# Moving 352 weight loads from SyncE's queue to ScalarE's in a fused attention and FFN kernel

## The chip, the cores and the metric

The kernel runs on one core of one Trainium2 chip. The metric is the device time of one execution in microseconds (us). A core has five engines that run side by side, each with its own instruction stream: TensorE (PE, matrix products; its weight loads are listed apart as PEld), VectorE (DVE), ScalarE (ACT), GpSimd (POOL) and SyncE (SP). Data moves between DRAM and the on-chip memory (SBUF) by DMA transfers, which an engine issues as an instruction of its stream and which sixteen DMA engines carry out. Matrix products land in PSUM, which here is used as eight banks. Engines wait for each other, and for transfers, on semaphores; an engine works through its instructions in order, so that whatever stands behind a waiting instruction waits too.

## The reference

Sixteen sequences of 512 tokens of width 512 go through one attention layer and one feed-forward layer (FFN):

```python
x = x + layernorm(attn(layernorm(x)))
x = x + layernorm(ffn(layernorm(x)))

def attn(h):                               # 16 heads of 32
    q = h @ Wq_down.T @ Wq_up.T
    c = h @ Wkv_down.T
    k, v = c @ k_up[h], c @ v_up[h]        # per head
    s = q @ k.T * SCALE - slope[h] * |i - j|
    return softmax(where(i >= j, s, -inf)) @ v @ Wo.T

def ffn(h):                                # I = 1408
    gate, up = split(h @ W_gu.T)           # W_gu, W_down: 4-bit codes x scales per 128 inputs
    y = (silu(gate) * up) @ W_down.T
    return y / sqrt(mean(y * y) + 1e-6)
```

## The kernel before

**The loop.** The kernel goes through 16 batches (one sequence each). A batch has an attention part of 16 pieces (4 groups of heads times 4 blocks of query rows) and an FFN part of 11 blocks of 128 inner columns. Nothing is written as a loop of the chip: every instruction of all batches stands in the program once.

**The order.** The kernel first lists all work as tasks. A task names the engine or engines that could run it, with two times for each (how long the engine is busy, when the result is there), a due time in units of a batch, and the buffers it reads and writes. The class `Plan` (L71) then puts all tasks in one order by a model of its own: over and over it takes, of all tasks that are ready, the one that could start first; with equal starts the one with the earlier due time. The order that comes out is the order of each engine's instructions. Three of its rules matter here. A task starts after its inputs with a hop of 150 ns between engines, 350 ns towards TensorE (`HOP`, `SLACK`). If the input is a transfer issued by SyncE and the task is TensorE's, the hop is 1000 ns (`LANDED`). A task of SyncE that needs a buffer starts no sooner than 4000 ns after that buffer came free (`VACANT`), so that its queue is not held by a wait for the buffer. The real times on the chip may differ from the model; the order stays.

**Transfers.** A load by SyncE is priced by `dma(us)` (L253): 450 ns of the issuing engine, and `us` until the data is there. In SyncE's stream stand, per batch from the second on: 4 loads of `xl` and 4 of `x` (rows of the input, L389 and L840); for each of the 16 attention pieces a store of the transposed probabilities to DRAM (`pd`, L793) and four loads that bring them back turned (`pT`, L798); for each of the 4 groups a store of the reciprocal row sums (`rd`, L742) and four loads that spread them (`rb`, L747); and for each of the 11 FFN blocks two loads of unpacked weights (`wi`, L889), one for gate and one for up. The first batch turns its probabilities on TensorE instead (L774) and unpacks the 4-bit codes once, into the DRAM tensor `w_gu` (stores at L562), from which all 352 loads of `wi` read. Results leave through GpSimd's queue (L983).

**The FFN block.** A load of `wi` is 256 KB: 128 partitions of 512 values. Four buffers take them in turn. Each is the weight operand of eight matmuls (L898): four slices of the input, each as a coarse and a fine part (`x2`) that add up in one PSUM bank. ScalarE empties the banks of the slices 0 and 2 with the scale (L912), VectorE those of 1 and 3, adding to the same tile (L919); GpSimd adds the two tiles (L925). Then come ScalarE's tanh (L932), VectorE's product for silu (L935) and GpSimd's product with up (L939), whose result `hT` is the operand of the down projection on TensorE (L947). In the order that the planner makes, the FFN of one batch lies among the attention of the next: TensorE alternates between gate/up products, down products (`py`), scores (`s`, L681) and attention products (`po`, L818). ScalarE's exponentials (L708) take the row minima `nmx` that VectorE finds (L693); VectorE also transposes the probabilities block by block (L791) before the store to DRAM.

**What the load waits for.** A load of `wi` waits for the matmuls that last read its buffer (a semaphore that TensorE raises) and, in the trace, often for an older transfer (one of eight semaphores that transfers raise).

The planner's rule for a start, and the load, are the lines that the change touches:

Of the kernel before, what the change touches and what calls it, by code (L numbers as in the profile page):

```python
# [29 lines left out]
PE, ACT, DVE, POOL, SP = "PE", "ACT", "DVE", "POOL", "SP"  # L30
# [29 lines left out]


class Task:
    __slots__ = ("on", "fn", "due", "deps", "wait", "next", "bufs", "end", "mode", "seq", "eng", "drains")

    def __init__(self, on, fn, due, mode, seq):
        self.on, self.fn, self.due, self.mode, self.seq = on, fn, due, mode, seq
        self.deps, self.next, self.bufs = set(), [], []
        self.wait, self.end, self.eng = 0, None, None


class Plan:  # L71
# [67 lines left out]
    def run(self, window):  # L139
        clock = {e: 0.0 for e in (PE, ACT, DVE, POOL, SP)}  # L140
        ready = {e: [] for e in clock}
        mode = "full"
        rest = sorted((t for t in self.tasks if PE in t.on), key=lambda t: t.due)
        at = 0
        for t in self.tasks:
            if t.wait == 0:
                for e in t.on:
                    ready[e].append(t)
        order = []

        def start(t, e, kept):
            s = clock[e]
            for d in t.deps:
                hop = 0.0 if d.eng == e else self.SLACK if e == PE else self.HOP
                if d.eng == SP and e == PE:
                    hop = self.LANDED
                s = max(s, d.end + hop)
            need = {}
            for b in t.bufs:
                if b.pool is not None and b.slot is None:  # L160
                    need[b.pool] = need.get(b.pool, 0) + 1
            for k, n in need.items():
                f = self.free[k]
                if len(f) < n + (kept if k == "bank" else 0):
                    return None
                s = max(s, f[n - 1][0] + (self.VACANT if e == SP and f[n - 1][0] else 0.0))
            return s

        left = len(self.tasks)
        while left:  # L170
            while at < len(rest) and rest[at].end is not None:
                at += 1
            limit = rest[at].due + window if at < len(rest) else float("inf")
            best = None
            for e, ts in ready.items():
                now, mine, kept = clock[e], None, 0
                if e == PE and ts:

                    first = min(ts, key=lambda t: (t.due, t.seq))
                    kept = sum(b.pool == "bank" and b.slot is None for b in first.bufs)  # L180
                for t in ts:
                    if t.due > limit:
                        continue
                    s = start(t, e, 0 if e != PE or t is first else kept)
                    if s is None:
                        continue
                    due = t.due
                    if e != PE:
                        due -= self.EARLY if t.drains else 0.0
                    elif t.mode != "full":  # L190
                        due -= self.STAY[mode != "full", t.mode == mode]
                    key = (max(s, now), due, t.seq)
                    if mine is None or key < mine[0]:
                        mine = key, t
                if mine is not None:

                    key, t = mine
                    cand = (key[0], key[1], key[2], e, t)
                    if best is None or cand[:3] < best[:3] or (
                        cand[:3] == best[:3] and t.on[e][1] < t.on[best[3]][1]  # L200
                    ):
                        best = cand
            assert best is not None, "the buffers do not suffice"
            s, _, _, e, t = best
            for o in t.on:
                ready[o].remove(t)
            for b in t.bufs:
                if b.pool is not None and b.slot is None:
                    b.slot = self.free[b.pool].pop(0)[1]
            busy, done = t.on[e]  # L210
            if e == PE and t.mode != mode:
                busy, done, mode = busy + self.SWITCH, done + self.SWITCH, t.mode
            clock[e] = s + busy
            t.end, t.eng = s + done, e
            for b in t.bufs:
                b.left -= 1
                b.last = max(b.last, t.end)
                if b.left == 0 and b.pool is not None:
                    self.free[b.pool].append((b.last + self.SLACK, b.slot))
                    self.free[b.pool].sort()  # L220
            for n in t.next:
                n.wait -= 1
                if n.wait == 0:
                    for o in n.on:
                        ready[o].append(n)
            order.append(t)
            left -= 1
        self.length = max(clock.values())
        return order
# [19 lines left out]
def pe(ns):  # L249
    return ns, ns + 250  # L250


def dma(us):  # L253
    return 450.0, us * 1000.0

# [1 line left out]
def attn_ffn_kernel(  # L259
# [15 lines left out]
    nc = tc.nc  # L275
# [41 lines left out]
    task = plan.task  # L317
# [91 lines left out]
    for w, src, due in ((w_qd, wqd, -0.38), (w_qu, wqu_t, -0.37)):  # L409
# [5 lines left out]
            due, writes=[w],  # L415
# [462 lines left out]
    def ffn(m):  # L878
# [3 lines left out]
        for i in range(NI):  # L882
            accs = []
            for half, kind in enumerate("gu"):
                acc = buf(kind, f"{kind}_{b}_{i}")
                add = buf("sum", f"{kind}2_{b}_{i}")
                wi = buf("wi", f"wi_{b}_{i}_{half}")
                task({SP: dma(4.5)},
                     lambda e, i=i, half=half, wi=wi: nc.sync.dma_start(  # L889
                         wi.t.bitcast(F32), w_gu[i, half]),  # L890
                     at - 0.1, reads=[(gu, (i, half))], writes=[wi])
                for c in range(ND):
                    o = half * ND + c
                    pm = buf("bank", f"p{kind}_{b}_{i}_{c}")

                    def f(e, wi=wi, c=c, pm=pm):
                        for n in range(2):
                            nc.tensor.matmul(  # L898
                                pm.t,
                                wi.t[:, c * P : (c + 1) * P],  # L900
                                m.x2.t[:, 1 - n, c, :],
                                start=n == 0,
                                stop=n == 1,
                            )

                    s = s_gu.t[:, i * NGU + o : i * NGU + o + 1]
                    to = acc if c < 2 else add
                    task({PE: pe(460)}, f, at, reads=[wi, m.x2], writes=[pm], hold=[to])
                    if c % 2 == 0:
                        task(  # L910
                            {ACT: act(512, 80)},
                            lambda e, to=to, pm=pm, s=s: nc.scalar.activation(  # L912
                                to.t, pm.t, AF.Copy, scale=s),
                            at, reads=[pm, s_gu], writes=[to],
                        )
                    else:
                        task(
                            {DVE: dve(512, 80)},
                            lambda e, to=to, pm=pm, s=s: nc.vector.scalar_tensor_tensor(  # L919
                                to.t, pm.t, s, to.t, ALU.mult, ALU.add),  # L920
                            at, reads=[pm, s_gu, to], writes=[to],
                        )
                    at += GU
                task({POOL: pool2(512)},
                     lambda e, acc=acc, add=add: nc.gpsimd.tensor_tensor(  # L925
                         acc.t, acc.t, add.t, ALU.add),
                     at, reads=[acc, add], writes=[acc])
                accs.append(acc)
# [10 lines left out]
                 lambda e, i=i, th=th, u=u: nc.gpsimd.tensor_tensor(  # L939
                     h_t.t[:, i, :], th.t, u.t, ALU.mult),  # L940
                 at, reads=[th, u], writes=[(h_t, i)])
        for t in range(NT):
            pm = buf("bank", f"py_{b}_{t}")
            for i in range(NI):
                task(
                    {PE: pe(858)},
                    lambda e, i=i, t=t, pm=pm: nc.tensor.matmul(  # L947
                        pm.t,
                        h_t.t[:, i, t * P : (t + 1) * P],
                        w_dn.t[:, i, :],  # L950
                        start=i == 0,
                        stop=i == NI - 1,
                    ),
# [3 lines left out]
            st, mv, rr, f = stats(lambda pm=pm: pm.t, f"y_{b}_{t}", at)  # L957
# [29 lines left out]
    for b in range(B):  # L987
# [21 lines left out]
        for n in range(NG * NT):  # L1009
            g, qb = divmod(n, NT)  # L1010
            due = b + FIRST + STEP * n
# [69 lines left out]
```

## Time and profile before

The median of three runs is 2514.41 us (2504.45 to 2514.54). All engine times come from one profiled execution.

| | before |
|---|---|
| profiled execution, us | 2511.75 |
| its span, first to last instruction, us | 2510.0 |
| mean granted TensorE clock | 0.985 |
| TensorE idle within the span, us | 91.5 |
| ScalarE idle within the span, us | 1036.9 |
| issues by SyncE's queue of `wi`, each 256 KB | 352 |
| issues of `pT` (64 to 256 KB) and `pd` (256 to 1024 KB) | 960 and 240 |
| bytes moved, MB, and mean rate, GB/s | 497.14, 198 |

How to read it: an engine's busy time is the time in which it runs instructions; waiting, branching and issuing of transfers do not count as busy. Idle time is the rest of the span. A line of the view of waits names the engine and tile that stood still, then what ended the wait, then the total in us, how many times, and the longest. A line of the timeline gives the start, the length, the engine, the source line and the tiles (out<-in), and in square brackets the idle time before it and what ended it. The granted clock is the share of full speed that TensorE was given; DMA share is the mean busy share of the sixteen engines, over 1 where their packets overlap. "SPq" is SyncE's queue.

### The profile page before, as it was taken

How to read it: one execution, taken by the hardware profiler on the slowest of the kernel's cores; microseconds unless marked ns; L12 is line 12 of the kernel's file. 1: busy time of each engine (PE TensorE's matmuls, PEld its weight loads, DVE VectorE, ACT ScalarE, POOL GpSimd, SP SyncE). 2: the span in 40 equal slices, each digit the busy share in tenths (PEclk: the TensorE clock that was granted, in tenths of full speed). 3: DMA queues.
4: the chain of work that ended last, by engine and by line, in shares of the span. 5: the costliest groups of instructions: out<-in, count | busy, mean ns of one | idle time of the engine just before them, and what ended most of it. 6: DMA issues, size and time to landing. Idle time of an engine off the chain costs nothing. (4 is left out here: it accounts for less than half of the span.)

```text
span 2510.0 us, 42451 instructions
## 1 busy us (share of the span) xinstructions
PE 2418.5 (96%) x13496; PEld 1334.7 (53%) x13496; DVE 1850.5 (74%) x4248; ACT 1473.1 (59%) x3484; POOL 1177.2 (47%) x1518
## 2 busy tenths in 40 slices
PE   7989999999999999999999999999999999999988
PEld 3546464555545555455554545555455554545554
DVE  4887786777768777687777867778686877767654
ACT  4875565655556566575565756556565665555443
POOL 1035454444444454454444544444454454544475
PEclk9999999999999999999999999999999999999999
DMA  7578696886868868696886978769687786967821
GB/s 239 172 201 227 178 245 184 206 224 177 219 187 235 210 179 233 165 247 189 216 211 179 246 181 227 212 170 245 160 236 197 205 226 167 237 167 194 215 67 47
DMA packets 487102, 497.14 MB, mean 198 GB/s; under 512 B 41568, under 2 KB 383456, under 8 KB 479200
## 3 DMA queue, kind: packets, MB, share of 16 engines
q1 hardware_dynamic: 481760, 477.65, 72.4%
q0 software_dynamic: 5120, 16.78, 1.8%
q8 instruction: 109, 1.79, 0.3%
q14 instruction: 113, 0.93, 0.1%
HBM read 313.42 MB, written 180.88 MB: 197 GB/s over the span
## 5 line engine op out<-in xcount | busy, mean ns | idle before, releaser
L947 PE MATMUL py<-w_dn,hT 128*128 128x512 f32 x1408 | 714.1, 610 | 0.8 <-POOL hT L939 0.8
L708 ACT ACTIVATE p<-p,nmx 128x128 f32<-128x128 f32 (+3 forms) x1024 | 564.3, 554 | 234.5 <-DVE nmx L693 221.7
L693 DVE CUSTOM_DVE_ANT_0 p<-s,dist 128x128 f32<-128x128 f32 (+3 forms) x1024 | 441.4, 485 | 93.6 <-PE s L681 90.9
L898 PE MATMUL pu<-x,wi 128*128 128x512 f32 x1408 | 466.8, 455 | 16.9 <-DMA wi<-w_gu 16.3
L898 PE MATMUL pg<-x,wi 128*128 128x512 f32 x1408 | 443.4, 441 | 25.9 <-DMA wi<-w_gu 16.1
L791 DVE STREAM_TRANSPOSE p<-p 128x512 f32<-128x512 f32 x240 | 360.3, 1501 | 41.5 <-ACT p L708 41.2
L925 POOL TENSOR_TENSOR u<-u,u 128x512 f32<-128x512 f32 x176 | 241.1, 1370 | 278.7 <-DVE u L919 277.3
L925 POOL TENSOR_TENSOR g<-g,g 128x512 f32<-128x512 f32 x176 | 229.1, 1301 | 275.1 <-DVE g L919 274.7
L898 PEld LDWEIGHTS pu<-x,wi 128*128 128x128 f32 x1408 | 267.2, 193 | 162.5 <-issue 92.0
L898 PEld LDWEIGHTS pg<-x,wi 128*128 128x128 f32 x1408 | 261.6, 191 | 164.6 <-issue 81.7
L912 ACT ACTIVATE u<-pu,s_gu 128x512 f32<-128x512 f32 x352 | 241.3, 686 | 177.6 <-PE pu L898 174.7
L947 PEld LDWEIGHTS py<-w_dn,hT 128*128 128x128 f32 x1408 | 248.2, 190 | 182.4 <-issue 152.1
L919 DVE SCALAR_TENSOR_TENSOR u<-pu,s_gu,u 128x512 f32<-128x512 f32 x352 | 259.2, 741 | 114.4 <-PE pu L898 80.8
L912 ACT ACTIVATE g<-pg,s_gu 128x512 f32<-128x512 f32 x352 | 238.9, 684 | 129.8 <-PE pg L898 114.5
L919 DVE SCALAR_TENSOR_TENSOR g<-pg,s_gu,g 128x512 f32<-128x512 f32 x352 | 258.9, 743 | 76.0 <-ACT g L912 47.1
L939 POOL TENSOR_TENSOR hT<-th,u 128x512 f32<-128x512 f32 x176 | 228.4, 1299 | 146.1 <-DVE th L935 136.0
L601 PE MATMUL pq<-xnT,w_q 128*128 128x512 f32 x512 | 233.6, 599 | 1.5 <-ACT w_q L440 1.5
L846 PE MATMUL pw<-w_o,atT 128*128 128x512 f32 x512 | 229.2, 596 | 0.0
L681 PE MATMUL s<-kT,qT 32*128 32x128 f32 (+3 forms) x2048 | 218.9, 482 | 1.1 <-ACT qT L623 1.1
L818 PE MATMUL po<-pT,v 128*32 128x128 f32 x5120 | 184.2, 278 | 14.3 <-DMA pT<-pd 11.1
L818 PEld LDWEIGHTS po<-pT,v 128*32 128x32 f32 x5120 | 128.2, 110 | 125.8 <-issue 87.5
L708 ACT ACTIVATION_READ_ACCUMULATOR p<-p,nmx 128x1 f32 x1024 | 194.9, 190 | 0.0
(94 smaller groups left out, 2397.2 us busy)
## 6 DMA issues: line engine op xcount, KB each, us to landing
wi<-w_gu SPq DMA_DIRECT2D x352, 256.0 KB
pd<-p SPq DMA_DIRECT2D x60, 1024.0 KB
pT<-pd SPq DMA_DIRECT2D x240, 256.0 KB
pd<-p SPq DMA_DIRECT2D x60, 768.0 KB
pT<-pd SPq DMA_DIRECT2D x240, 192.0 KB
pd<-p SPq DMA_DIRECT2D x60, 512.0 KB
pT<-pd SPq DMA_DIRECT2D x240, 128.0 KB
xl<-x_in SPq DMA_DIRECT2D x64, 256.0 KB
```

The lines of the kernel that those rows point to most:

```text
L601: nc.tensor.matmul(pm.t, lhs(c), rhs(c), start=c == 0, stop=c == n - 1)
L693: lambda e, j=j: nc.vector.tensor_tensor_reduce(part(m, p, j), runs(s[j].t[:, :w]), runs(dist.t[:, L - w :]), -SLOPES[g * HPG + j], 3.4e38 ...
L708: lambda e, j=j: nc.scalar.activation(part(m, p, j), part(m, p, j), AF.Exp, bias=nmx.t[:, j : j + 1], scale=-1.0, accum_out=sums.t[:, qb * ...
L791: task({DVE: dve(row, 0.07 * row)}, lambda e: nc.vector.transpose(flat(p.t), flat(p.t)), due, reads=[p], writes=[p])
L818: nc.tensor.matmul(po.t[j * HD : (j + 1) * HD, qb * P : (qb + 1) * P], m.v.t[:, kb, h * HD : (h + 1) * HD], p_t.t[:, kb, :, j, :], start=k ...
L846: nc.tensor.matmul(pm.t, m.at.t[:, g, t * P : (t + 1) * P], w_o.t[:, g, :], start=g == 0, stop=g == NG - 1,)
L898: nc.tensor.matmul(pm.t, wi.t[:, c * P : (c + 1) * P], m.x2.t[:, 1 - n, c, :], start=n == 0, stop=n == 1,)
L912: lambda e, to=to, pm=pm, s=s: nc.scalar.activation(to.t, pm.t, AF.Copy, scale=s),
L919: lambda e, to=to, pm=pm, s=s: nc.vector.scalar_tensor_tensor(to.t, pm.t, s, to.t, ALU.mult, ALU.add),
L925: lambda e, acc=acc, add=add: nc.gpsimd.tensor_tensor(acc.t, acc.t, add.t, ALU.add),
L939: lambda e, i=i, th=th, u=u: nc.gpsimd.tensor_tensor(h_t.t[:, i, :], th.t, u.t, ALU.mult),
L947: lambda e, i=i, t=t, pm=pm: nc.tensor.matmul(pm.t, h_t.t[:, i, t * P : (t + 1) * P], w_dn.t[:, i, :], start=i == 0, stop=i == NI - 1,),
```

## The change

The loads of `wi` are issued by ScalarE (`nc.scalar.dma_start`) instead of SyncE (`nc.sync.dma_start`), with the same source, destination and size. In the planner their price on the issuing engine is 100 ns instead of 450; the 4.5 us until the data is there, the due time and the buffers are the same. The two rules that asked for SyncE by name (`LANDED` towards TensorE, `VACANT` for a buffer) now ask whether a task's result comes more than 1000 ns after its engine is done with it, which holds for every transfer and for no computation. For SyncE's other transfers the rules give what they gave before. GpSimd's store of the result (1000 and 3000 ns) now counts too, but TensorE waits for none of them and none takes a new buffer.

```diff
 class Task:
-    __slots__ = ("on", "fn", "due", "deps", "wait", "next", "bufs", "end", "mode", "seq", "eng", "drains")
+    __slots__ = ("on", "fn", "due", "deps", "wait", "next", "bufs", "end", "mode", "seq", "eng", "drains", "moves")
...
         self.wait, self.end, self.eng = 0, None, None
+        self.moves = all(done > busy + 1000 for busy, done in on.values())
...
-                if d.eng == SP and e == PE:
+                if d.moves and e == PE:
                     hop = self.LANDED
...
-                s = max(s, f[n - 1][0] + (self.VACANT if e == SP and f[n - 1][0] else 0.0))
+                s = max(s, f[n - 1][0] + (self.VACANT if t.moves and f[n - 1][0] else 0.0))
...
-def dma(us):
-    return 450.0, us * 1000.0
+def dma(us, busy=450.0):
+    return busy, us * 1000.0
...
-                task({SP: dma(4.5)},
-                     lambda e, i=i, half=half, wi=wi: nc.sync.dma_start(
+                task({ACT: dma(4.5, 100.0)},
+                     lambda e, i=i, half=half, wi=wi: nc.scalar.dma_start(
                          wi.t.bitcast(F32), w_gu[i, half]),
                      at - 0.1, reads=[(gu, (i, half))], writes=[wi])
```

## The prediction

> **What bounds the kernel now.** I read the shares by engine first, then who waited for whom on TensorE, then SyncE's own waits, then the granted clock around the longest waits, then one such place instruction by instruction.
>
> ```profile
> PE 2418.5 (96%) x13496; PEld 1334.7 (53%) x13496; DVE 1850.5 (74%) x4248; ACT 1473.1 (59%) x3484; POOL 1177.2 (47%) x1518
> PEclk9999999999999999999999999999999999999999
> ```
>
> TensorE carries the kernel: 96% busy, none of the others above 74%. The span is 2510.0 us, so all its idle time is 91.5 us. What ends that idle time (total us, times, longest):
>
> ```profile
> PE pu L898 <- DMA wi<-w_gu: 16.3, 13, 4.2
> PE pg L898 <- DMA wi<-w_gu: 16.1, 9, 3.1
> PE po L818 <- DMA pT<-pd: 11.1, 7, 2.8
> PE ptf L491 <- DVE y L476: 8.4, 2, 6.6
> ...
> PE pg L898 <- ACT g L912: 2.3, 6, 0.4
> ```
>
> The 22 waits for the gate/up weights (tile wi) are the largest item: 32.4 us. TensorE hardly ever waits for ScalarE. They cost more than their length, because the clock falls after them. In the table by stretch (length, then busy us of PE, PEld, DVE, ACT, POOL, then granted clock, DMA share, GB/s):
>
> ```profile
> 485.30:492.10 6.80, 5.91 (x16) 2.84 (x16) 2.66 (x6) 2.48 (x7) 1.49 (x2) 0.50 0.90 256
> ...
> 1240.00:1248.00 8.00, 7.83 (x36) 4.22 (x34) 7.74 (x16) 6.28 (x15) 3.81 (x3) 1.00 1.12 206
> 1248.00:1256.00 8.00, 5.79 (x26) 3.86 (x27) 4.70 (x12) 2.54 (x6) 1.27 (x1) 0.62 1.06 363
> ```
>
> Between 165 and 2400 us the clock record has nine stretches at 0.50: three of 3.4 us and six of 6.8 us, 51 us in all, so 25.6 us of full-speed work is lost. Each begins inside a wait of TensorE or at most 0.8 us after one. Two (184.9 and 485.3 us; 10.2 us long) go with a wait for wi alone; six (34.0 us) with a wait for pT of 1.3 to 2.8 us and one for wi of 0.7 to 1.3 us right behind it; the last (2308.0) with a wait of 3.4 us that the trace puts on VectorE.
>
> Why wi is late: SyncE's queue, in order, and one of the six places.
>
> ```profile
> SPq L793 <- DVE p L791: 498.9, 148, 10.3
> ...
> SPq L889 <- PE pg L898: 90.2, 55, 29.6
> SPq L889 <- PE pu L898: 50.2, 73, 2.4
> SPq L889 <- DMA pT<-pd: 37.0, 57, 1.4
> ```
>
> ```profile
> 1237.75 0.43 SPq L889 DMA_DIRECT2D wi<-w_gu  x1
> 1238.22 6.15 SPq L798 DMA_DIRECT2D pT<-pd  x8
> 1244.47 0.57 SPq L889 DMA_DIRECT2D wi<-w_gu  x1
> ```
>
> ```profile
> 1249.11 0.65 PE L818 MATMUL po<-pT,v 128*32 128x128 f32 x16 [1.28 <-DMA pT<-pd]
> 1250.85 1.19 PE L898 MATMUL pu<-x,wi 128*128 128x512 f32 x2 [1.10 <-DMA wi<-w_gu]
> ```
>
> The buffer of this load was free at 1237.0 us (end of the matmuls that read its last content), but eight pT issues took 6.15 us ahead of it, so it left 7.5 us later and TensorE stood still at 1249.76. Two or three such places recur in nearly every batch.
>
> **The change, part by part.** Bytes, packets and matmuls stay. 352 issues move from SyncE to ScalarE; the planner's rules for them (4 us after a buffer came free, 1 us from landing to TensorE) stay; its price on the issuer falls from 450 to 100 ns.
>
> *The waits for wi.* Where would ScalarE issue? I laid the planner's order of the kernel before (order alone) on the trace, and took for each load the end of the ScalarE task that stands ahead of it. For the 348 loads whose buffer had been used before, that end comes 4.5 us (median) after the buffer is free, 5.4 at the 90th percentile; SyncE issued at 3.8 and 7.4. At the place above it is the end of the tanh that starts at 1240.32, 1241.0 instead of 1244.47. So an ordinary load leaves about a microsecond later, a late one 1.5 to 3.5 us earlier. From issue to the last packet the loads now take 2.1 us at best and 4.3 us in the median, with the rest of SyncE's ring ahead of them. With 3.6 us, between the two and nearer the median because the sixteen DMA engines stay shared, 4.4 us of TensorE's waiting is left: gain 28 us; with the median's 4.3, 8.0 us is left: gain 24. Bounds: 32.4 and nothing.
>
> The Trainium skill speaks against a gain here: "DMA: Bandwidth & Descriptors", section "Issuing engines are not separate DMA queues", says that transfers of all issuers end on the same 16 engines and interleave, and that a second issuer saves only issue time. The DMA share of 1.12 and 1.06 above agrees that the engines are full there. By that rule landing stays at 4.3 us and the gain is 24 instead of 28 us; the larger part is SyncE's lateness, which the rule leaves standing.
>
> *The clock.* The two stretches behind wi alone go: 5 us. Of the six behind pT and wi I count half, since the wait for pT alone was shorter than both together: 8.5 us. Gain 14 us; bounds 0 and 25.6.
>
> *SyncE.* It loses 352 issues of 378 ns (its median; 319 to 2160) and 140 us of waiting for PE at L889 (90.2 + 50.2), so pd, pT, rb and xl leave sooner. That could shorten the 11.1 us behind pT; wi's packets beside them could lengthen it. I count nothing, with ±11 us.
>
> *ScalarE: the issues.* No ScalarE issue is in the trace; nearest are SyncE's. 352 x 0.378 us = 133 us, against 1037 us that ScalarE is idle. Behind an issue queue L912's drains, L708's exponentials and L932's tanh; TensorE waits for the bank, VectorE (L919) for the tile.
>
> *ScalarE: a new wait.* A transfer signals one of eight semaphores in turn (100 to 107 in the trace), and 333 of the 352 loads are preceded by a wait for an older, unrelated transfer:
>
> ```profile
> L889 SPq DMA_DIRECT2D wi<-w_gu x352: 319/378/2160, 98.5 to 2467.5; - x176
> L889 SPq EVENT_SEMAPHORE  x333: 17/17/28, 176.1 to 2465.2; - x167
> ```
>
> If the turn runs over both queues, ScalarE will stand until a transfer of SyncE eight places ahead has landed. Laid on the trace as above that is 84 us over 54 loads, 36 of them over 1 us, the longest 4.1; for the buffer itself ScalarE would never wait. If each queue has its own turn it is nothing. I take the 84.
>
> *ScalarE: what reaches TensorE.* Issue and wait, 217 us, fall at places where ScalarE mostly has a hole: beyond the idle time right there only 69 us remain as a delay. TensorE runs ahead of the drains: of 1089 banks that ScalarE emptied, half were taken again 1.8 us or more later, 225 within 1.0 us and 67 within 0.5 us. I let a quarter of the delay through, 17 us: the share of banks with under 1.0 us (21%), rounded up. Bounds 0 and 69. If the holes and the banks gave no cover, the whole 217 us would lie on the path.
>
> *Sum*: -28 - 14 + 17 = -25 us. The profiled execution took 2511.75 us (span 2510.0, 1.75 around it), so 2487; the median of three is 2514.41, 2.7 above, and the same step from it gives 2489. The likeliest case's own range: 32 + 26 + 11 gained and nothing lost, down to 24 gained and 17 lost: 2445 to 2507.
>
> **Rivals.**
>
> *B, ScalarE becomes the brake: slower.* For: its pass through SyncE's landings joins two queues that ran apart; SyncE stood 498.9 us for VectorE's transposes, up to 10.3 us at once, and any such lag now holds the drains; ScalarE is busy 5.2 to 6.3 of 8 us in the dense stretches. Against: its 41% idle time and the banks. Price: all 69 us, and as much clock lost behind the new stops as is lost now (0 gained), against 28 gained: +41, 2555; with half of the 69, +7. It decides from where a load costs TensorE 0.12 us on average (42 us of gain over 352 loads).
>
> *C, the DMA engines are the limit: no gain.* wi comes earlier, pT as much later, and TensorE's 28 us wait at L818 instead; the clock falls as before; ScalarE's 17 us are lost. For: share over 1.0 at the very places, and pT already waits there. Against: the mean share over the span is 0.75 (72.4, 1.8, 0.3 and 0.1% by queue), so there is room between the crowded stretches. 2514 + 17 = 2531; without ScalarE's loss 2514.
>
> *D, the change does not do what it says.* ScalarE reaches the issue behind its own waits (174.7 us for pu, 221.7 for VectorE's minima) and the loads are as late as in SyncE's queue. Against: the order above. Then only the 17 us count, or less: 2514 to 2531.
>
> **How the numbers follow.** Chances: A (forecast) 0.50, B 0.24, C 0.16, D 0.10. A measurement of this kernel tells about 0.5% (12.6 us) from no change. Faster by more: nearly all of A, and small shares of C and D where ScalarE costs little: 0.52. Within: the weak ends of A, B and C: 0.15. Slower: most of B, more than half of C and D: 0.33. The time is A's, 2489. The range, 2448 to 2545, takes A's own and reaches up to B's price, leaving out about a tenth on each side.
>
> **What would show it.** Right, if PE's waits for wi fall under 8 us, the 0.50 stretches between 165 and 2400 drop from nine to three to six, and PE's waits for ScalarE (L912) and the holds of ScalarE at L889 stay under 25 us of TensorE's time. Issues on ScalarE should last about 0.38 us. Wrong, if waits of ScalarE for pT or pd appear in the hundreds of us and TensorE waits for g, u or s behind them (B); if PE's waits for pT grow by some 28 us (C); or if the issue comes over 7 us after its buffer is free at the same three places (D). A different order from the planner, since the load's price there changes, could move all of this by some microseconds a batch, and nothing in the trace of before bounds that.

## The result, and the profile after

The changed kernel is slower: 2611.86 us, the median of four runs (2600.35 to 2619.03), against 2514.47 (2504.45 to 2515.04) for the kernel before in the same series. The ratio is 1.0387, 95% interval 1.0368 to 1.0406, so about 97 us are lost. The profiled execution took 2600.35 us, its span is 2598.6.

Lines moved by one or two in the changed file: the load of `wi` is L891 (L889 before), its matmuls L900 (L898), the loads of `pT` L799 (L798), the stores of `pd` L794 (L793), their matmuls `po` L819 (L818).

The page first: the share of TensorE, the granted clock in 40 slices, and the queues (packets, MB, share of sixteen DMA engines).

```profile
PE 2428.9 (93%) x13496; PEld 1356.7 (52%) x13496; DVE 1856.8 (71%) x4258; ACT 1468.2 (56%) x3474; POOL 1177.9 (45%) x1518
...
PEclk9999999999899999999999999999999999999999
...
q1 hardware_dynamic: 431072, 385.35, 55.8%
q10 hardware_dynamic: 50688, 92.30, 13.2%
```

The loads did move: 92.30 MB now run in a queue of their own. TensorE's idle time grew from 91.5 to 169.7 us (2598.6 - 2428.9). Its busy time grew by 10.4 us, though the work is the same. The view of waits on TensorE says where the idle time is:

```profile
PE po L819 <- DMA pT<-pd: 111.5, 37, 6.0
PE pg L900 <- DMA wi<-w_gu: 7.7, 7, 1.9
...
PE pu L900 <- DMA wi<-w_gu: 1.2, 2, 0.8
```

The waits for wi fell from 32.4 to 8.9 us. The waits for pT rose from 11.1 to 111.5. The two together make +76.9 us, nearly all of the 78.2 by which TensorE stands longer. The clock went the same way: between 165 and 2400 us there are 23 stretches at 0.50 instead of nine, 109 us instead of 51.

Why is pT late? SyncE's own waits:

```profile
SPq L794 <- DVE p L792: 528.9, 121, 11.6
SPq L799 <- DMA wi<-w_gu: 242.2, 105, 7.3
...
SPq L799 <- DMA pd<-p: 117.2, 48, 5.7
SPq L794 <- DVE rowsums L738: 88.6, 12, 10.4
SPq L794 <- DMA wi<-w_gu: 59.7, 29, 6.7
...
SPq L748 <- DMA wi<-w_gu: 18.7, 9, 4.7
...
SPq L743 <- DMA wi<-w_gu: 9.6, 5, 3.8
```

SyncE, which no longer loads wi and reads none of it, stands for landings of wi at the lines that issue pT, pd, rb and rd: 330.2 us in these four rows, 334 with the smaller one. In the kernel before it was 14 us, nearly all of it in three rows:

```profile
SPq L889 <- DMA wi<-w_gu: 6.5, 10, 1.5
SPq L798 <- DMA wi<-w_gu: 4.4, 10, 0.9
...
SPq L793 <- DMA wi<-w_gu: 2.1, 7, 0.5
```

The reason is the eight completion semaphores. In the trace every transfer of SyncE or ScalarE signals one of 100 to 107 in turn, one turn for both, and none is issued before the earlier transfer on the same semaphore has landed.

One place shows it. The timeline (start, length, engine, line, operation), SyncE, then ScalarE, then TensorE:

```profile
1279.53 11.93 SPq L799 DMA_DIRECT2D pT<-pd  x8
...
1283.22 0.33 ACTq L891 DMA_DIRECT2D wi<-w_gu  x1
...
1295.07 2.79 PE L819 MATMUL po<-pT,v 128*32 128x128 f32 x48 [3.55 <-DMA pT<-pd]
```

Eight issues of pT take 11.93 us; a run of eight took 6.15 in the kernel before, at 1238.22. The trace's records inside that line, with the semaphore that each transfer signals:

```
start     end       issuer   transfer   semaphore
1281.66   1282.30   SyncE    pT         101
1282.60   1283.16   SyncE    pT         103
1283.22   1283.55   ScalarE  wi         105
1289.38   1289.94   SyncE    pT         105
1289.99   1290.60   SyncE    pT         106
1290.90   1291.46   SyncE    pT         107
```

SyncE was ready for its next pT at 1283.16. That pT's semaphore, 105, belongs first, in the turn, to ScalarE's load of 1283.22, and SyncE stood 6.21 us until the load had landed. Its last pT left at 1290.90, and TensorE waited 3.55 us for it. Of the 111.6 us that TensorE waits for pT (all waits over 0.1 us), 106.0 us, 33 of 38 waits, lie behind such a place: SyncE had stood for a wi over 0.5 us (4.7 in the median of the longest) within the 8 us before the issue of that pT. Of all 960 loads of pT 42% lie behind such a place, so that 95% of the waiting is not what chance would give.

The clock pays too, in the table by stretch (length, then busy us of PE, PEld, DVE, ACT, POOL, then granted clock, DMA share, GB/s):

```profile
1286.00:1294.00 8.00, 5.03 (x21) 2.29 (x19) 7.75 (x19) 6.68 (x18) 2.53 (x2) 0.98 0.89 229
1294.00:1302.00 8.00, 6.93 (x61) 5.76 (x62) 2.77 (x5) 2.40 (x5) 1.17 (x1) 0.60 0.83 282
```

TensorE begins to stand in the first 8 us, and in the next 8 us its mean clock is 0.60 of full speed.

### The profile page after: what moved, and what is told of

Same layout as the page of the kernel before. It is cut to its first block, busy times and chain, and to the rows that moved or that the text cites. A ratio compares the mean times of both kernels' runs of the same rounds, so it can differ in the third digit from the quotient of the medians.

```text
span 2598.6 us, 42193 instructions
## 1 busy us (share of the span) xinstructions
PE 2428.9 (93%) x13496; PEld 1356.7 (52%) x13496; DVE 1856.8 (71%) x4258; ACT 1468.2 (56%) x3474; POOL 1177.9 (45%) x1518
## 3 DMA queue, kind: packets, MB, share of 16 engines
q10 hardware_dynamic: 50688, 92.30, 13.2%
## 4 chain that ended last, share of the span: by engine, by line
PE 76%; DMA 15%; ACT 3%; DVE 2%; SPq 2%; issue 1%; POOL 1%; ACTq 0%; POOLq 0%; DVEq 0%
PE py L949 21%; PE pg L900 11%; PE pu L900 10%; PE pw L847 8%; PE pq L602 8%; DMA pT<-pd 6%; DMA wi<-w_gu 6%; PE po L819 6%; PE s L682 5%; PE pv L602 2%; PE pc L602 2%; PE pk L602 2%; SPq L799 1%; PE ptf L492 1%; DMA w_dn<-gup 1%
## 5 line engine op out<-in xcount | busy, mean ns | idle before, releaser
L900 PE MATMUL pu<-x,wi 128*128 128x512 f32 x1408 | 466.5, 453 | 6.9 <-DVE g L921 5.7
L900 PE MATMUL pg<-x,wi 128*128 128x512 f32 x1408 | 460.9, 456 | 11.8 <-DMA wi<-w_gu 7.7
L900 PEld LDWEIGHTS pg<-x,wi 128*128 128x128 f32 x1408 | 272.1, 197 | 154.3 <-issue 77.3
L900 PEld LDWEIGHTS pu<-x,wi 128*128 128x128 f32 x1408 | 264.5, 192 | 153.8 <-issue 78.8
L819 PE MATMUL po<-pT,v 128*32 128x128 f32 x5120 | 193.2, 290 | 114.5 <-DMA pT<-pd 111.5
L819 PEld LDWEIGHTS po<-pT,v 128*32 128x32 f32 x5120 | 138.4, 114 | 207.6 <-issue 150.5
```

Of the source, the lines that this page charges most:

```text
L819: nc.tensor.matmul(po.t[j * HD : (j + 1) * HD, qb * P : (qb + 1) * P], m.v.t[:, kb, h * HD : (h + 1) * HD], p_t.t[:, kb, :, j, :], start=k ...
L900: nc.tensor.matmul(pm.t, wi.t[:, c * P : (c + 1) * P], m.x2.t[:, 1 - n, c, :], start=n == 0, stop=n == 1,)
```

## The experiments

Three theories. **T**: the shared turn of the eight semaphores makes SyncE's pT and pd wait for landings of wi. **D**: two queues beside each other crowd the sixteen DMA engines, so pT and pd land later. **O**: the planner's new order (the load costs 100 ns of ScalarE instead of 450 of SyncE) loses time whoever issues. Ratios are to the kernel before on the same chip.

**1. Order and queue apart.** The first kernel is the changed one, its order kept, but SyncE issues:

```diff
-                     lambda e, i=i, half=half, wi=wi: nc.scalar.dma_start(
+                     lambda e, i=i, half=half, wi=wi: nc.sync.dma_start(
```

> The order that the planner makes for the changed kernel, but the 352 loads issued by SyncE at the places in its stream that this order gives them. Theory T (the eight semaphores that transfers raise in turn are shared by both queues, so that SyncE's pT loads stand until one of ScalarE's wi loads has landed): the loss goes away, 2500 to 2530 us, TensorE's waits for pT under 25 us, its waits for wi back at 20 to 45 us. Theory D (two queues share the DMA engines, and wi's packets delay pT's): the same, as there is one queue. Theory O (the new order itself asks for pT too early): no change from the changed kernel, 2595 to 2620 us, waits for pT near 110 us.

Measured: 2548.47 us, ratio 1.0149 (1.0133 to 1.0164). TensorE's waits:

```profile
PE pg L900 <- DMA wi<-w_gu: 70.7, 17, 5.6
PE po L819 <- DMA pT<-pd: 7.4, 3, 3.1
...
PE pu L900 <- DMA wi<-w_gu: 3.2, 2, 1.9
```

pT is as short as T said, but wi is 73.9 us, and the time lies above T's range. So the order is a loss of its own: 36 us (2548.47 - 2512.35) when SyncE issues; a likely reason is that the planner no longer counted the loads in SyncE's queue.

The second is the kernel before, its order kept, but ScalarE issues:

```diff
-                     lambda e, i=i, half=half, wi=wi: nc.sync.dma_start(
+                     lambda e, i=i, half=half, wi=wi: nc.scalar.dma_start(
```

> The order of the kernel before (planner untouched, load priced on SyncE), but the 352 loads issued by ScalarE where that order has them. T: slow like the changed kernel or worse, 2570 to 2640 us; SyncE stands over 150 us for landings of wi, TensorE over 60 us for pT. D: slow too, 2570 to 2620, but without long waits of SyncE for wi. O: as before, 2500 to 2530.

Measured: 2565.18 us, ratio 1.0215 (1.0197 to 1.0234), a little under the range that T gave. TensorE's wait for pT, then SyncE's waits:

```profile
PE po L818 <- DMA pT<-pd: 88.4, 31, 6.7
```

```profile
SPq L798 <- DMA wi<-w_gu: 152.6, 69, 6.9
...
SPq L747 <- DMA wi<-w_gu: 84.1, 34, 6.0
SPq L793 <- DMA wi<-w_gu: 47.5, 21, 6.9
```

With the order of the kernel before, ScalarE's queue alone brings the whole picture: SyncE stands 303 us for wi, and TensorE waits 77 us more for pT. Neither part alone is the 97 us; each is a share of it.

**2. Another set of semaphores.** Transfers of GpSimd signal 111 to 118, so its loads take no turn away from SyncE. First the changed kernel with the planner's own order for GpSimd:

```diff
-                task({ACT: dma(4.5, 100.0)},
-                     lambda e, i=i, half=half, wi=wi: nc.scalar.dma_start(
+                task({POOL: dma(4.5, 1000.0)},
+                     lambda e, i=i, half=half, wi=wi: nc.gpsimd.dma_start(
```

> The changed kernel with the 352 loads issued by GpSimd (planner price 1000 ns there), whose transfers raise semaphores of another set: a queue of their own, but no shared turn. T: SyncE's waits for landings of wi fall from 334 us to under 20, TensorE's for pT to under 30 and for wi under 15 us, 2480 to 2525 us. D: wi's packets still stand beside pT's, waits for pT stay near 100 us, 2580 to 2620. O: much as the changed kernel, 2580 to 2620.

Measured: 2511.0 us, ratio 0.9993 (0.9983 to 1.0002); SyncE's waits for wi are gone, TensorE's for pT are 32.7 us, a little over T's 30. But its order is a third one. Experiment 4 shows that orders differ by more than what is to be explained, so the time of this run proves nothing for T; that SyncE no longer stands does speak for it.

The kernel before, its order kept:

```diff
-                     lambda e, i=i, half=half, wi=wi: nc.sync.dma_start(
+                     lambda e, i=i, half=half, wi=wi: nc.gpsimd.dma_start(
```

> The kernel before with its order kept and only the issuer of the gate/up loads changed, to GpSimd; against the run with the same order and ScalarE as issuer (2565). T (SyncE and ScalarE share one turn of eight completion semaphores, GpSimd's queue has others): SyncE's waits for wi fall from 303 us to under 10, TensorE's waits for pT from 88 us to under 45, and the time to 2480-2515. D (two queues beside each other crowd the DMA engines, whoever issues): pT stays over 70 us and the time is 2540-2580. O (the planner's order is what costs): this order has no loss of its own, so nothing beyond the kernel before with a time of 2505-2520 by chance of the same sum.

Measured: 2540.52 us, ratio 1.012 (1.0089 to 1.0152). SyncE's waits for wi are gone as T said, but the time misses T's range by 25 us and just falls into D's, and pT lies between the two:

```profile
PE po L818 <- DMA pT<-pd: 53.6, 26, 6.2
PE pg L898 <- DMA wi<-w_gu: 15.0, 15, 2.1
```

The changed kernel, its order kept:

```diff
-                     lambda e, i=i, half=half, wi=wi: nc.scalar.dma_start(
+                     lambda e, i=i, half=half, wi=wi: nc.gpsimd.dma_start(
```

> The changed kernel with its order kept task for task (the planner still prices the load on ScalarE), only the issuer is GpSimd, so that the loads no longer take a turn among the eight semaphores of SyncE and ScalarE. T (shared turns): SyncE's waits for wi fall from 334 us to under 5; from the end of VectorE's transpose to the issue of pd 0.6-0.9 us in the mean instead of 1.9; TensorE's waits for pT 20-60 us instead of 111; time 2515-2560. O (the order of the changed kernel asks for pT too early, whoever issues): pT stays over 90 us and the time over 2585. D (loads beside SyncE's transfers slow them): pT lands later than in the changed kernel, and if that is what costs, pT stays over 90 us too.

Measured: 2574.69 us, ratio 1.0248 (1.0218 to 1.0278). No wait of SyncE for wi; pd leaves 0.64 us after the transpose; pT is 65.4 us, above T's 60, and the time 15 us above T's range, 10 below that of O:

```profile
PE po L819 <- DMA pT<-pd: 65.4, 37, 3.8
PE pu L900 <- DMA wi<-w_gu: 17.5, 16, 2.1
PE pg L900 <- DMA wi<-w_gu: 12.4, 11, 2.7
```

These five make a table of two orders and three issuers, as ratios to the kernel before:

| order | SyncE issues | ScalarE issues | GpSimd issues |
|---|---|---|---|
| of the kernel before | 1 | 1.0215 | 1.0120 |
| of the changed kernel | 1.0149 | 1.0387 | 1.0248 |

The order costs 1.3 to 1.7% in every column. ScalarE's queue costs 2.2 and 2.4%, GpSimd's 1.2 and 1.0% (in per cent of the time of the kernel before). What differs between the issuers stands in SyncE's path, worked out from the records of transfers for the 240 stored blocks of probabilities (means in us; "issued" is the start of the issue, "landed" the last packet):

```
issuer, order         transpose   pd issued   pd landed     first to      fourth pT   whole
                      to pd       to landed   to first pT   fourth pT     to landed
SyncE,   before         0.80        4.24        10.74         2.14          4.25       22.17
ScalarE, before         2.29        3.77        10.96         2.61          3.91       23.54
GpSimd,  before         0.72        4.89        10.44         2.09          4.82       22.95
SyncE,   changed        0.75        4.33        11.33         2.07          4.22       22.70
ScalarE, changed        1.93        3.85        11.55         2.69          3.92       23.93
GpSimd,  changed        0.64        4.92        10.76         2.12          4.96       23.39
```

With ScalarE as issuer SyncE issues pd 1.2 to 1.5 us later and needs half a microsecond more for four pT: the standing of T. The transfers themselves land sooner than before, so D is not what ScalarE's queue costs. With GpSimd as issuer the issues are on time, and pd and pT land 0.6 to 0.7 us later each: there D is seen, and it probably takes back part of what T frees. GpSimd was also 180 us busier with the loads to issue (1357.6 us against 1177.2, and 1360.1 against 1177.9), and no run tells the two apart. Nor do ScalarE's issues delay the work that feeds the store: from the end of the scores to the end of VectorE's transpose it is 7.49 us in the kernel before and 7.55 with ScalarE issuing in the same order.

**3. The dose of T: runs with more or less of it.** The changed kernel with ScalarE's loads planned 1000 instead of 4000 ns after their buffer came free:

```diff
-                s = max(s, f[n - 1][0] + (self.VACANT if t.moves and f[n - 1][0] else 0.0))
+                s = max(s, f[n - 1][0] + ((1000.0 if e == ACT else self.VACANT) if t.moves and f[n - 1][0] else 0.0))
```

> The changed kernel with the planner's distance between a freed wi buffer and its load cut from 4 to 1 us for ScalarE's loads alone, so that they leave about 3 us sooner. T: the loads land sooner and hold SyncE less: its waits for wi fall from 334 us to 100 to 200, TensorE's for pT from 111 to 40 to 70 us, 2540 to 2585 us; some waits of ScalarE for the buffer are new. D: the same bytes beside pT, no change, 2590 to 2625. O: no change beyond 1%.

Measured: 2573.47 us, ratio 1.024 (1.0215 to 1.0264). Time and pT (72.5 us) are in T's range, but SyncE's waits for wi did not fall (336 us in all); this row alone is over T's 200 us:

```profile
SPq L799 <- DMA wi<-w_gu: 244.0, 94, 5.9
```

Had SyncE waited for a ScalarE that issues late, an earlier place of the loads in the order would have cut the waits. It is not so: of the 334 us in the changed kernel only 17 pass before ScalarE has issued the load; 317 pass while it is under way (4.1 us from issue to the end of the wait in the median). SyncE waits for the transfer, not for ScalarE. The planner made an order of its own for this run too, so its shorter time is not shown to come from T.

The changed kernel with each load in two halves:

```diff
-                     lambda e, i=i, half=half, wi=wi: nc.scalar.dma_start(
-                         wi.t.bitcast(F32), w_gu[i, half]),
+                     lambda e, i=i, half=half, wi=wi: [nc.scalar.dma_start(
+                         wi.t.bitcast(F32)[r : r + 64], w_gu[i, half][r : r + 64]) for r in (0, 64)],
```

> The changed kernel with every gate/up load issued by ScalarE as two transfers of 64 partitions, the same bytes: 704 turns of the semaphores instead of 352. T: SyncE meets a semaphore of a wi transfer more often, its waits for wi rise from 334 us to 450-700, TensorE's waits for pT from 111 us to 130-220, and the time to 2630-2720. D (bytes beside each other on the DMA engines): the bytes are the same, pT stays at 100-125 us and the time at 2595-2625. Against both: smaller transfers land sooner, and then SyncE's waits could shrink, to under 300 us, with a time under 2600.

Measured: 2665.13 us, ratio 1.062 (1.0595 to 1.0645). The time is in T's range, pT (125.4 us) a little under it, SyncE's waits far under it:

```profile
SPq L799 <- DMA wi<-w_gu: 215.1, 112, 6.3
```

With the smaller rows it is 339 us, hardly more than in the changed kernel. And an issue of half a tile took 0.552 us instead of 0.326, so ScalarE spent 389 us on issuing instead of 115. ScalarE's idle time that ends with a landing of wi is 58.6 us now (3.4 in the changed kernel). The run tells against D (the same bytes, 53 us more), but not whether the turns or the issues cost them.

The kernel before, its order kept, with up's loads on ScalarE and gate's on SyncE:

```diff
-                     lambda e, i=i, half=half, wi=wi: nc.sync.dma_start(
+                     lambda e, i=i, half=half, wi=wi: (nc.scalar if half else nc.sync).dma_start(
```

> The order of the kernel before; gate's 176 loads stay with SyncE, up's 176 go to ScalarE. Half the dose of the run with all 352 on ScalarE in this order (2565, SyncE's waits for ScalarE's wi 303 us, pT 88 us). T: 110-200 us of SyncE's waits, pT 30-60 us, wi 5-25 us, time 2525-2555. If two queues beside each other cost by themselves (D), landing of pd and pT grows; T says that they land no later than in the kernel before, 4.2 us each in the mean, and that the loss is in the issue of pd: 1.3-1.7 us after the transpose against 0.8 before and 2.3 with all loads.

Measured: 2586.69 us, ratio 1.0298 (1.0279 to 1.0316): half the dose is worse than the whole one. TensorE's waits, then SyncE's:

```profile
PE pg L898 <- DMA wi<-w_gu: 63.4, 17, 10.1
PE po L818 <- DMA pT<-pd: 34.5, 18, 3.7
```

```profile
SPq L798 <- DMA wi<-w_gu: 160.1, 43, 7.6
...
SPq L747 <- DMA wi<-w_gu: 86.7, 21, 7.1
SPq L389 <- DMA wi<-w_gu: 23.0, 13, 5.3
```

SyncE stands 289 us, nearly as long as with all 352 loads on ScalarE, so T's sum by halves was wrong. pd and pT land no later (3.92 and 3.98 us) and pd leaves 2.23 us after the transpose, as with all loads. What is new is that gate's loads now sit in the queue that stands: TensorE waits 63.4 us for them, and 60.3 of these, 13 of 17 waits, lie behind a place where SyncE had stood for a wi over 0.5 us within the 8 us before it issued the load (40% of all its loads do). The same standing, with another victim, is T's mechanism and not D's.

The changed kernel with the old price in the planner:

```diff
-                task({ACT: dma(4.5, 100.0)},
+                task({ACT: dma(4.5)},
```

> The changed kernel with the planner's price of an issue on ScalarE put back to 450 ns: a third order with ScalarE as issuer. T (the queue costs 50-65 us in whichever order, by the shared turns): SyncE's waits for wi 280-360 us, pd issued 1.8-2.5 us after the transpose in the mean, pT 70-120 us, time 2555-2620. If it is the order with the low price that makes the loss, pT falls under 40 us and the time to 2500-2530, with SyncE still standing.

Measured: 2587.78 us, ratio 1.0311 (1.0291 to 1.0331); SyncE's waits for wi 362 us, just over T's range, pd 1.76 us after the transpose, pT 89.8 us. All 33 waits for pT (92.1 us; the view counts one of them as issue) lie behind a place where SyncE stood for a wi. The low price was not the cause of the main loss; at most the 0.8% between this run and the changed kernel is its share.

These four runs do not make a scale of T. SyncE stood 289 to 362 us in all of them, while the time went from 2573 to 2665 us, so the sum of the standing alone does not set the time.

**4. Versions that might beat both.** The changed kernel in which the planner picks SyncE or GpSimd for each load:

```diff
-                task({ACT: dma(4.5, 100.0)},
-                     lambda e, i=i, half=half, wi=wi: nc.scalar.dma_start(
+                task({SP: dma(4.5), POOL: dma(4.5, 1000.0)},
+                     lambda e, i=i, half=half, wi=wi: (nc.sync if e == SP else nc.gpsimd).dma_start(
```

> The planner may issue each gate/up load from SyncE (450 ns) or from GpSimd (1000 ns), whichever can start it first. T: no load takes a turn away from SyncE that SyncE does not itself issue, so SyncE's waits for ScalarE's wi are gone; wi waits of TensorE under 25 us, pT under 30 us, time 2475-2515. D: the loads on GpSimd's queue still slow pd and pT by about half a microsecond each as in the runs with all loads there; time 2505-2545.

Measured: 2526.76 us, ratio 1.0066 (1.004 to 1.0091). SyncE issued 189 of the loads, GpSimd 163. pT is 15.0 us as T said, but wi 29.5, over T's 25, and the time lies above T's range and in D's: no gain.

The first GpSimd version (2511 us) with a later landing of pd and pT in the planner's model:

```diff
-        task({SP: dma(5.5 + w / 200)}, lambda e: nc.sync.dma_start(d.t, flat(p.t)), due,
+        task({SP: dma(6.1 + w / 200)}, lambda e: nc.sync.dma_start(d.t, flat(p.t)), due,
...
-                {SP: dma(5 + w / 160)},
+                {SP: dma(5.6 + w / 160)},
```

> The version with all loads on GpSimd in the planner's own order (2511) with the planner told that pd and pT land 0.6 us later, as they did in that run. If the 33 us of waiting for pT left there come from landings that are later than planned, they fall under 20 us and the time to 2485-2505; if the planner's estimate matters little, 2500-2520.

Measured: 2580.18 us, ratio 1.0271 (1.0252 to 1.029), far above both ranges. pT stays at 33.9 us; new waits of TensorE for VectorE came up (26.4 us at L900, for the tile u).

The same version with the price of an issue nearer to its length:

```diff
-                task({POOL: dma(4.5, 1000.0)},
+                task({POOL: dma(4.5, 600.0)},
```

> The version with all loads on GpSimd (2511 at a price of 1000 ns) with the price at 600 ns, near the 570 ns that an issue took there. T: SyncE's waits for wi under 5 us and pd issued 0.6-0.9 us after the transpose, as in every run with GpSimd as issuer. The time tells how much the planner's order alone moves a kernel with the same queues: 2500-2525 if little, up to 2580 if it moves as much as the two other orders did (2541 and 2575).

Measured: 2666.99 us, ratio 1.0629 (1.0605 to 1.0653), far outside the range. The issuer, the queue and the work are those of the version at 2511 us; only a number in the planner's model differs, and it moves the time by 156 us:

```profile
PE po L819 <- DMA pT<-pd: 76.4, 23, 5.9
PE s L682 <- DVE g L921: 62.9, 13, 6.1
```

SyncE issued pd 0.91 us after the transpose, with no wait for wi, so T plays no part in it. No version beats the kernel before.

## Why the prediction was wrong

Forecast: faster, 2489 us, in a range of 2448 to 2545. Measured: 2611.86. Step by step:

- **The waits for wi: right.** -28 us were forecast, 4.4 left; -23.5 came, 8.9 left. The number is near the step's other end, a gain of 24 with landings that stay at 4.3 us, but not for that reason: from issue to the last packet the loads took 4.3 us in the median before, 3.2 in the changed kernel and 3.2 with ScalarE issuing in the order of the kernel before, where only 1.4 us of waiting for wi are left. The rule of the Trainium skill weighed there ("DMA: Bandwidth & Descriptors", "Issuing engines are not separate DMA queues": a second issuer saves issue time only) was read to mean that landing stays as it is. These landings do not bear that out.
- **SyncE: the step that failed.** It said that pd, pT, rb and xl leave sooner, "I count nothing, with ±11 us". Measured: +100.4 us of TensorE's waits for pT. SyncE was given back its issue time (352 issues) but stands 334 us for landings of wi, and pd leaves 1.1 us later than before, not sooner.
- **The new wait: the right object, priced in one direction.** The prediction saw the eight semaphores and that one turn might run over both queues. It then priced only ScalarE's standing for SyncE's transfers, 84 us over 54 loads. By the trace ScalarE stands some 19 us for pT, pd and wi in all, 8.7 of them at one place; the kernel before has 9.9 us in all. The wait went the other way: SyncE issues four or eight transfers at once, catches up with the turn, and meets a load that ScalarE has issued and that has not landed. The sum that was made over ScalarE's 352 issues had to be made over SyncE's 1710 too.
- **ScalarE's issues: a fair size, harmless.** 352 x 0.326 = 115 us instead of 133, from these rows (shortest, median and longest ns):

```profile
L891 ACTq DMA_DIRECT2D wi<-w_gu x352: 325/326/1326, 95.7 to 2560.3; - x176
L891 ACTq EVENT_SEMAPHORE  x209: 17/17/38, 180.9 to 2536.3; - x105
```

  Nothing of the +17 us was seen: the view of TensorE's waits has no row for ScalarE's g or u, and one of 0.8 us for its tanh.
- **The clock: wrong in sign.** -14 us forecast. The stretches at 0.50 follow waits of TensorE, whoever causes them, and grew by 58 us, 29 us of full-speed work. Some of that time lies inside the waits counted above, so it isn't added to them; TensorE's busy time shows 10.4 us of it. In the changed kernel all 23 stretches begin inside a wait or at most 1.2 us after one, and 20 of these waits are for pT. Counting half of the six stretches behind pT and wi as gone had a weak ground, too: in two of them (1854.0 and 2157.8 us) the clock had fallen after a wait for pT alone, of 2.14 and 2.82 us, before the wait for wi began.
- **The planner's order: left out.** The prediction said only that it could move all by some microseconds a batch. It is 1.5% with SyncE as issuer, 36 us or 2.3 a batch, and by experiment 4 an order can be worth 156.

Of the rivals, B had the mechanism (joining two queues that ran apart) but put the brake on ScalarE and the price at 41 us. C had the symptom, the wait that moves to pT, but not the cause: pd and pT land sooner than before. D is out: the loads came in time.

**What stays open.** The queue's share on ScalarE is 2.2 to 2.4%. That SyncE's standing reaches TensorE there is shown by the records, and with GpSimd as issuer, where the standing is absent, the loss is 1.0 and 1.4% smaller. How much would be left if ScalarE's transfers had semaphores of their own on the same hardware queue was not tried; GpSimd's queue removes the standing but brings later landings with it. Why the changed order is worse by much the same with all three issuers isn't settled either: with SyncE it shows as waits for wi, with the others mostly for pT.

## What to carry to other kernels

Before a transfer is moved to another issuer, list what the two issuers will then share besides the DMA engines, here the completion semaphores, and price the wait in both directions; here the issuer with bursts was the one that was held. Look at the semaphore numbers in the trace: two issuers that signal the same ones in one turn, as here, can hold each other. And where a planner writes the order, compare old and new issuer in one and the same order first, since the order alone can move more than the change.

## What the runs showed of the hardware

- In these programs eight semaphores (100 to 107) served SyncE's and ScalarE's transfers together, and 111 to 118 GpSimd's. The Trainium skill ("DMA: Bandwidth & Descriptors", "Why a DMA increments its semaphore by 16 and not by 1") asks for one semaphore for each transfer in flight, since two on one semaphore can be taken for landed too early. The trace agrees: in no place are two transfers under way on one semaphore, and with eight of them the price was the wait for the older transfer, 334 us of SyncE.
- With the loads in ScalarE's queue SyncE's own transfers landed sooner (pd 3.77 us instead of 4.24, in the same order), and so did the loads (3.2 us instead of 4.3 in the median); with the loads in GpSimd's queue pd landed later (4.89). The bytes are the same. SyncE, which stood, issued its own transfers further apart with ScalarE as the second issuer, so the runs do not show what the queue does by itself.
- An issue of 128 partitions took ScalarE 0.326 us in the median (SyncE 0.378, GpSimd 0.577), of 64 partitions 0.552.
